# A message-passing layer on one core: the third chunk's lists merged at once, the last roots of the tail together, nine tiles fetched by rows, stores and list loads moved later on SyncE

## The chip, the cores and the metric

The kernel runs on one core of one Trainium2 chip. The metric is the device time of one execution in microseconds; the median over three executions is given, and one further execution was profiled. The engines are called PE (TensorE), DVE (VectorE), ACT (ScalarE), POOL (GpSimd) and SP (SyncE, which here only starts DMAs).

## The reference

A graph layer with a residual and a layer norm: 12,500 nodes, 400,000 edges sorted by target `dst`, 128 features, float32.

```python
# cut to what matters
rbf  = exp(-(distances[:, None] - centers) ** 2 / (2 * width * width))        # 50 centres
cut  = 0.5 * (cos(pi * distances / 10) + 1) * (distances <= 10)
W    = (silu(rbf @ fw1 + fb1) @ fw2 + fb2) * cut[:, None]
messages = (h[src] @ pw + pb) * W
agg  = segment_sum(messages, dst, num_segments=12500)
layer = h + (silu(agg @ mw1 + mb1) @ mw2 + mb2)
out  = layernorm(x + layer)                                                    # h is x
```

The weights of the edges are spread wide, so most edges lie beyond the distance of 10, have `cut` 0 and add nothing.

## The kernel before

**Packing.** The edges come in 7 chunks. For each chunk DVE finds which edges count and moves them together within a row by shifts that are doubled (`shift`, `moving`, `resting`: L509 to L519), and GpSimd scatters the rows into a DRAM area `packed` with one indirect DMA per chunk (L494). SyncE loads them back as lists of pairs (L821), and `unpack` merges the two halves of each pair on DVE (`two`, L839/840; `part`, L858; `f_src`, L869), turns them on PE (L902) and casts them to `srci`, the numbers of the source nodes for the gathers (L907), and likewise to `dl` and `cut`. The lengths go to DRAM (`near_d`, L896) and come back as `d`, ready for the radial basis (L1067). The kept edges fill 139 tiles of 512 edges (`NL`); chunk c holds the tiles from QB[c], with QB = (0, 13, 24, 46, 69, 91, 114, 141).

**The loop over tiles** (`octs`, from L1489). For tile q:
- `fetch` (L1048): GpSimd gathers four quarters of 128 rows of `proj` (the projected nodes, `h @ pw + pb`, in DRAM) with one indirect DMA each, into one of 21 buffers of the `quad` kind. It runs many tiles ahead of the rest where it can.
- `first` and `silu` (L1103, L1109), on PE and ACT, for two tiles at once; `second` (L1117, L1120) on PE.
- `message` (L1131) on DVE multiplies the gathered rows and PE's result.
- `place` (`hot`, L1143) on DVE builds a 0/1 matrix times `cut`, and `sum_up` (L1163) on PE adds up the messages by target; `add` (L1196) on DVE puts the sums into `aggT`.

In the tiles of `SINGLY` the first quarter isn't gathered: `one_by_one` lets SyncE read 32 row numbers at a time into registers (L1034) and copy each of the 128 rows by a DMA of its own (L1038, 0.5 KB) into one of four slots of `dl_0`; the message then takes two steps (L1129 for that quarter, L1131 for the rest). A_ROW is the pace, in us per row, at which these copies are written into the order.

**Finished nodes.** Blocks of up to 512 nodes go through `node_first` (L1204, L1205, then the silu L1209), `node_second` (L331, L334), `node_stats` (L1225 adds x, L1230 takes mean and variance), `deviations` (L1237 to L1241, a square root on ACT), `scales` (L1248, L1249) and `normalize` (L1260 on DVE, L1263 on ACT, then the store L173). Square root and silu lie in different table sets of ACT, so each change loads a table. Sixteen columns of statistics (four blocks) share one root.

**Order.** All engines run in order, and their order is written by hand: the generator keeps a model clock, the packing of later chunks is a coroutine that is woken when `awake[c]` has passed on that clock, and `pack_until` mixes its pieces in among the tiles. The end has its own script: `READY` says behind which tile a last block starts (block 80 nine tiles before the end, 84 six, 88 five, 90 three, 93 two, 95 last), and `keep_busy(n)` issues n matmuls that nobody uses into the bank of `ph` (L1352).

```python
READY = {80: 9, 84: 6, 88: 5, 90: 3, 93: 2}
...
            if q == NL - k:
                if t0 == 84:
                    keep_busy(8)
                node_first(t0)
```

Of the kernel before, what the change touches and what calls it, by code (L numbers as in the profile page):

```python
# [43 lines left out]
NL = 139  # L44
# [23 lines left out]
CLEAR_C = 2  # L68
PACK_US = 1.5
EARLY_US = 7  # L70
SINGLY = (22, 45, 62, 67, 86, 102, 118, 133)
A_ROW = .58
AT_ONCE = 32
FROM_BANK = 3

# [8 lines left out]
def kernel(  # L84
# [37 lines left out]
    nc = tc.nc  # L122
# [18 lines left out]

    x_sb, loaded = {}, [0]

    def load_x(t0, n=None):
        t = x4_sb[loaded[0] % X_BUFS]
        loaded[0] += 1
        node_dma(t0, t, x, False, n)
        x_sb[t0] = t
# [19 lines left out]
    def node_dma(t0, sb, dr, store, n=None, eng=nc.sync):  # L168

        for a, m, k in alike(rows(t0, n)):  # L170
            d = dr[(t0 + a) * P:(t0 + a) * P + m * k].rearrange("(p t) f -> p t f", p=k)
            s = sb[:k, a:a + m]
            eng.dma_start(d, s) if store else eng.dma_start(s, d)  # L173
# [164 lines left out]
    srci = keep.tile([P, NP, 2], I32, name="srci")  # L338
# [61 lines left out]
    clock = [3.2]  # L400
    pool = [0.0]
    there_at = {}
    summed = {}
    awake = [0.0] * NC_
# [49 lines left out]
    def parts(n):  # L454

        return [(a, b) for a, b in ((0, n // 16 * 16), (n // 16 * 16, n)) if b > a]
# [236 lines left out]
    def pack(c):  # L693
# [73 lines left out]
        for b in range(bits):  # L767
# [11 lines left out]
            n, k = reach(c, b, bits), 1 << b  # L779
            early = "two" not in pa_of  # L780
# [22 lines left out]
            yield one(n)  # L803

        yield from columns(c, nodes, r_d, first, 0, CAP, at_i)
        awake[c] = pool[0] + (2.2 if c == 1 else 3.0)
        awake[0] = 0.0
        yield 0
        yield from unpack(c)
# [1 line left out]
    def unpack(c):  # L811
# [15 lines left out]
        if c < 2:  # L827
            more_ = np_ if c == 0 else SPILL
            also = work.tile([P, 2, QE], F32, name="s", bufs=3).bitcast(I32)
            listed(also, 0, more_, 3, LISTS)  # L830
        awake[c] = max(awake[c], clock[0]) + (6 if c < 1 else 3.5 if c < 2 else 4.0)
        yield 0
        def alike_in(k):
            nc.vector.tensor_tensor(pair[:more_, :LISTS - 3, k::2], pair[:more_, :LISTS - 3, k::2],
# [2 lines left out]
        def one_of(to, k):  # L837

            nc.vector.tensor_tensor(to, pair[:np_, 0, k::2], pair[:np_, 1, k::2], OP.bitwise_or)  # L839
            nc.vector.tensor_tensor(to, to, pair[:np_, 2, k::2], OP.bitwise_or)  # L840
# [40 lines left out]
        def later(more=0.0):  # L881

            if c or known[0] >= DIRECT // QT:
                awake[c] = clock[0] + (5.0 if known[0] >= QB[c + 1] else 1.0 if c == 0 else 2.5) + more
                return 0.0
            return 0.5
# [3 lines left out]
        def lengths():  # L890

            if c < 2:
                alike_in(1)
            one_of(length, 1)
            for a, b in parts(np_):
                nc.sync.dma_start(near_d[p0 + a:p0 + b], length[a:b].bitcast(F32))  # L896
            stored.add(c)

        def to_places(f, to):
            t, tp = turned()  # L900
            for j in range(2):
                nc.tensor.transpose(tp[:, j, :np_], f[:, j * P:(j + 1) * P], ident[:np_, :np_])  # L902
            if to is srci:
                lengths()
                yield 1.4 if c < 2 else 0.8
            yield later(-2.0 if c == 1 and to is srci else 0.0)
            nc.vector.tensor_copy(to[:, p0:p0 + np_, :].rearrange("p r j -> p j r"),  # L907
                                  tp[:, :, :np_])
            back(t)
# [334 lines left out]
    def scales(group, both, s):  # L1244

        n = s.shape[1]
        r, by = (work.tile([P, 16], F32, name=k, bufs=2)[:, :n] for k in ("rs", "by"))
        nc.vector.reciprocal(r, s)  # L1248
        nc.vector.scalar_tensor_tensor(by, both[:, :, 0], -0.5, r, op0=OP.mult, op1=OP.mult)  # L1249
        at = 0  # L1250
        for t in group:
            ready.append((t, r[:, at:], by[:, at:]))
            at += len(rows(t))

    def normalize(t0, rs, by, on=(), eng=nc.sync):

        y = x_sb.pop(t0)
        for k, m in enumerate(rows(t0)):
            if k in on:
                nc.vector.tensor_scalar(y[:m, k, :], y[:m, k, :], rs[:m, k:k + 1], by[:m, k:k + 1],  # L1260
                                        op0=OP.mult, op1=OP.add)
            else:
                nc.scalar.activation(y[:m, k, :], y[:m, k, :], AF.Identity, bias=by[:m, k:k + 1],  # L1263
                                     scale=rs[:m, k:k + 1])
        node_dma(t0, y, out, True, eng=eng)

    ready = []

# [22 lines left out]
        begin[t0] = [at_q, at_q + 1, at_q + (4 if NODES + 24 < at_q < NL - 20 else 3)]  # L1291
        at_q += 2 if at_q % 4 == 1 else 3
    early = list(begin)
    assert begin[early[-1]][2] <= NL - 3

    def nodes(q):

        if deep:
            scales(*deep.pop())
        for _ in ready[:1 if q < NL - 6 else 2]:  # L1300
            normalize(*ready.pop(0))
        for k, t0 in enumerate(early):
            if begin[t0][0] - 5 == q:
                load_x(t0)
            if begin[t0][2] == q:
                if k % 4 == 0:
                    st_of[0] = statistics()
                node_stats(t0, st_of[0][:, k % 4 * 4:])
                if k % 4 == 3:
                    deep.append(deviations(early[k // 4 * 4:k + 1], st_of[0]))  # L1310
            if begin[t0][1] == q:
                node_second(t0)
            if begin[t0][0] == q:
                node_first(t0)
        for k, t0 in enumerate(TAIL):
            if q == NL - 9 + k:
                load_x(t0)
        if q == NL - 7:
            st_of[3] = statistics()
            node_stats(80, st_of[3])  # L1320
        if q == NL - 4:
            node_stats(84, st_of[3][:, 4:])
        if q == NL - 3:
            node_stats(88, st_of[3][:, 8:])
            dev_of.append(deviations([84, 88], st_of[3][:, 4:]))
            nc.scalar.activation(warm, half_pi, AF.Silu)
        if q == NL - 2:
            node_second(90)
            for k in (1, 2):
                st_of[k] = statistics()  # L1330
            scales(*dev_of.pop(0))
            for _ in (84, 88):
                normalize(*ready.pop(0))
# [3 lines left out]
    def tail(q):  # L1337

        for t0, k in READY.items():
            if q == NL - k:  # L1340
                if t0 == 84:
                    keep_busy(8)
                assert done_to(2 * added(q + 1)) >= (t0 + TAIL[t0]) * P
                node_first(t0)
            if q == NL - k + 1 and t0 in (80, 84, 88):
                node_second(t0)
# [142 lines left out]
    for q in range(NL - 1):  # L1489
# [39 lines left out]
        for k in now:  # L1529
            if q < NL - 2:  # L1530
                base_of(k, (1,))
            if q == NL - 7 and k == now[0]:
                deep.append(deviations([80], st_of[3]))
                nc.scalar.activation(warm, half_pi, AF.Silu)
            add(k)
# [24 lines left out]
    node_second(95)  # L1560
    early_dev = deviations([90, 93], st_of[1])
    node_stats(95, st_of[2], lambda: scales(*early_dev))
    last_dev = deviations([95], st_of[2])
    for _ in (90, 93):
        normalize(*ready.pop(0))
    scales(*last_dev)
    normalize(*ready.pop(0), on=(0, 1), eng=nc.scalar)

# [110 lines left out]
```

## Time and profile before

| | |
|---|---|
| median of 3 executions | 734.89 us (734.77 to 734.94) |
| profiled execution, its own time | 736.03 us |
| its span | 734.3 us |
| mean granted TensorE clock | 0.920 |
| DMA bytes moved, mean rate | 91.37 MB, 124 GB/s |

The span is the stretch that the profile covers, from the first to the last recorded instruction; 1.7 us of the profiled execution's time lie outside it. Its page gives for each engine the busy time, then slices of the span, the DMA queues, the chain of work that ended last, and the costliest groups of instructions. In a group's row the first number behind the bar is the busy time in us and the second the mean in ns of one; the number behind the second bar is the time in us that the engine stood idle just before these instructions, with what ended it (`issue`: nothing that the profile shows). A row of single instructions has the start, the duration, the engine, the line, what is written and read, how many follow each other, and in brackets the idle time before.

### The profile page before, as it was taken

The page shows a single profiled execution, that of the slowest core. Times are in us where ns is not written, and L with a number is a line of the kernel's source. Part 1 is how long each engine was busy: PE and PEld are TensorE (multiplying, and loading weights), DVE is VectorE, ACT ScalarE, POOL GpSimd, SP SyncE. Part 2 cuts the span into 40 slices and gives each one's busy share as a digit, 9 for nine tenths or more (in the row PEclk, how much of TensorE's full clock was granted, in tenths as well). Part 3 has the DMA queues.
Part 4 walks back from the last instruction along what each step waited for, and adds up shares of the span by engine and source line. Part 5 has one row for each costly group of instructions (what it writes and reads, how often), then busy time and mean ns, then how long its engine had stood idle before and what let it go on. Part 6 is the DMA issues. An engine that isn't in the chain of part 4 may idle for free.

```text
span 734.3 us, 13663 instructions
## 1 busy us (share of the span) xinstructions
PE 590.7 (80%) x3527; PEld 461.9 (63%) x3527; DVE 560.2 (76%) x1737; ACT 403.0 (55%) x574; POOL 533.5 (73%) x569
## 2 busy tenths in 40 slices
PE   6877876797888787878698969999978787778684
PEld 5766565676666665667476758777656565565463
DVE  8899798878878997989889957877455555556663
ACT  6557634274444864536457256859456644653763
POOL 7777777577777777777777777777777777777750
PEclk9999687999999998989989989999998999999886
DMA  8995442233234323343233343535333433343231
GB/s 267 313 318 189 143 128 73 89 120 99 76 110 128 95 85 101 99 127 88 83 111 113 96 134 97 155 120 151 110 113 94 127 124 98 98 142 116 79 114 53
DMA packets 53103, 91.37 MB, mean 124 GB/s; under 512 B 13824, under 2 KB 20576, under 8 KB 53018
## 3 DMA queue, kind: packets, MB, share of 16 engines
q1 hardware_dynamic: 34466, 53.20, 21.8%
q0 software_dynamic: 17840, 36.77, 18.1%
q8 instruction: 29, 0.48, 0.3%
q10 hardware_dynamic: 712, 0.46, 0.2%
q14 instruction: 56, 0.46, 0.2%
HBM read 74.59 MB, written 15.79 MB: 123 GB/s over the span
## 4 chain that ended last, share of the span: by engine, by line
DMA 13%; PE 13%; DVE 11%; POOL 9%; issue 6%; ACT 3%; DVEq 1%; POOLq 0%; SPq 0%; ACTq 0%
DMA quad<-proj,srci 11%; POOL quad L1048 9%; PE ph L1103 3%; PE bank L1120 3%; PE sums L1163 3%; DVE hot L1143 2%; DVE quad L1143 2%; PE bank L1205 1%; DVE msg L1131 1%; DMA pair<-packed 1%; DVE aggT L1196 1%; DVE st L1230 1%; DVEq L1173 1%; ACT x L1263 1%; DMA packed<-line,at_i 1%
## 5 line engine op out<-in xcount | busy, mean ns | idle before, releaser
L1048 POOL DMA_INDIRECT quad<-proj,srci x421 | 400.9, 952 | 132.5 <-issue 94.9
L1120 PEld LDWEIGHTS bank<-fw_sb,s 128*128 128x128 f32 x1112 | 159.7, 207 | 72.9 <-issue 65.8
L1109 ACT ACTIVATE s<-ph 128x1024 f32<-128x1024 f32 x70 | 71.2, 1017 | 179.7 <-PE ph L1103 179.5
L1120 PE MATMUL bank<-fw_sb,s 128*128 128x128 f32 x1112 | 159.7, 291 | 0.0
L1103 PE MATMUL ph<-rbf,w_sb 102*128 102x512 f32 x278 | 145.9, 651 | 6.7 <-ACT s L1109 3.5
L1163 PEld LDWEIGHTS sums<-hot,msg 128*128 128x128 f32 x816 | 107.6, 198 | 55.9 <-issue 27.5
L1143 DVE TENSOR_SCALAR hot<-iota_n,dl,cut 128x80 f32<-128x80 f32 (+4 forms) x408 | 109.1, 341 | 27.5 <-PE sums L1163 25.3
L1163 PE MATMUL sums<-hot,msg 128*128 128x80 f32 (+4 forms) x816 | 110.4, 280 | 14.2 <-DVE msg L1131 13.9
L1117 PE MATMUL bank<-fb_b,ones_b 96*128 96x512 bf16 x139 | 56.5, 406 | 54.8 <-DVE msg L1131 34.1
L1048 POOL DMA_INDIRECT x<-proj,srci x79 | 75.5, 955 | 24.2 <-issue 19.8
L1131 DVE TENSOR_TENSOR msg<-bank,quad 128x512 f32<-128x512 f32 (+1 forms) x82 | 55.5, 677 | 45.9 <-DMA quad<-proj,srci 41.6
L1103 PEld LDWEIGHTS ph<-rbf,w_sb 102*128 102x128 f32 x278 | 52.6, 211 | 46.1 <-issue 38.3
L1196 DVE TENSOR_TENSOR aggT<-aggT,sums 128x80 f32 (+4 forms) x209 | 53.9, 258 | 32.4 <-PE sums L1163 11.1
L1094 ACT ACTIVATE rbf<-d,rbf_bias,rbf_scale 102x512 f32<-102x512 f32 x70 | 56.3, 804 | 19.6 <-DMA d<-near_d 19.6
L1048 POOL DMA_INDIRECT quad<-in_x_dram,srci x48 | 46.7, 974 | 15.7 <-issue 11.9
L334 PEld LDWEIGHTS bank<-pw_sb,xT 128*128 128x128 f32 (+1 forms) x292 | 43.0, 212 | 9.4 <-issue 6.0
L1109 ACT ACT_TABLE_LOAD x36 | 46.2, 1283 | 0.6
L1095 ACT ACT_TABLE_LOAD x35 | 44.9, 1283 | 0.6
L1095 ACT ACTIVATE rbf<-rbf 102x512 f32<-102x512 f32 x70 | 44.1, 630 | 1.5
L334 PE MATMUL bank<-pw_sb,xT 128*128 128x128 f32 (+1 forms) x292 | 43.3, 296 | 0.7 <-ACT xT L984 0.6
L1163 PE MATMUL sums<-quad,quad 128*128 128x128 f32 (+3 forms) x296 | 40.8, 284 | 2.9 <-DVE quad L1131 2.8
L1143 DVE TENSOR_SCALAR quad<-iota_n,dl,cut 128x128 f32<-128x128 f32 (+3 forms) x148 | 40.6, 353 | 3.3 <-issue 2.1
(272 smaller groups left out, 791.4 us busy)
## 6 DMA issues: line engine op xcount, KB each, us to landing
d<-near_d SPq DMA_DIRECT2D x70, 256.0 KB
dl<-proj SPq DMA_DIRECT2D x1024, 0.5 KB
x<-in_x_dram SPq DMA_DIRECT2D x46, 256.0 KB
quad<-proj,srci POOLq DMA_INDIRECT x421
proj<-hp SPq DMA_DIRECT2D x24, 256.0 KB
out_dram<-x SPq DMA_DIRECT2D x22, 256.0 KB
r_d<-in_edge_weight_dram SPq DMA_DIRECT2D x5, 256.0 KB
r_dst<-in_dst_dram SPq DMA_DIRECT2D x5, 256.0 KB
```

Of the source, the lines that this page charges most:

```text
L334: nc.tensor.matmul(to[:m, k, :], lT[:, k * P:k * P + m], w, start=False, stop=(k == a + c - 1))
L1048: ins = nc.gpsimd.indirect_dma_start(out=got[:, j, :], out_offset=None, in_=proj if table is None else table, in_offset=bass.IndirectOffse ...
L1094: nc.scalar.activation(rbf[:u], d[:u], AF.Square, bias=rbf_bias[:u], scale=rbf_scale[:u])
L1095: nc.scalar.activation(rbf[:u], rbf[:u], AF.Exp, scale=-1.0 / (2.0 * width * width))
L1103: nc.tensor.matmul(ph[:, h, :], w1_sb[:2 * KR, h, :], rbf[:2 * KR], start=True, stop=True)
L1109: nc.scalar.activation(s[:, :n], ph[:, :n], AF.Silu)
L1117: nc.tensor.matmul(pu, ones_b[:, :P], bias_b["fb2"].rearrange("k j f -> k (j f)"), start=True, stop=False)
L1120: nc.tensor.matmul(pu[:, j * H:(j + 1) * H], s[:, j * P:(j + 1) * P], fw2_sb, start=False, stop=(j == QT - 1))
L1131: nc.vector.tensor_mul(msg[:, a:b, :], pu_of[q].rearrange("p (j f) -> p j f", j=QT)[:, a:b, :], got_of[q][:, a:b, :])
L1143: nc.vector.tensor_scalar(hot[:, j, :wide(q)], iota_n[:, :wide(q)], dl[:, at[0], at[1]], cut[:, at[0], at[1]], op0=OP.is_equal, op1=OP.mult)
L1163: ins = nc.tensor.matmul(pa[:, k * W:k * W + wide(q)], msg[:, j, :], hot[:, j, :wide(q)], start=(j % n == 0), stop=(j % n == n - 1))
L1196: nc.vector.tensor_add(to, to, pa[:, k * W:k * W + wide(q)])
```

## The change

1. `SINGLY` has nine tiles in place of eight, at other places: 22, 43, 58, 68, 83, 96, 109, 122, 136 for 22, 45, 62, 67, 86, 102, 118, 133. `A_ROW` goes from 0.58 to 0.515.
2. Chunk 2 is the third chunk. Its merge is woken as soon as its lists have been asked for (`awake` plus 0 in place of plus 4), and its `srci` is written 2.5 earlier on the model clock. In the order of DVE its `two`, `f_src`, `length` and `srci` now stand behind the first shift (L515) of chunk 3 and ahead of the message of tile 5, where they stood behind that tile's sums.
3. For chunks 3 to 6 the lists are loaded 8 later than the scatter on the model clock, not 3, and the lengths are stored behind the pause `later()`, not ahead of it. The scatters of chunks 3 to 6 move in POOL's order from ahead of the gathers (36,0), (52,0), (68,0), (82,0) (tile, quarter) to ahead of (38,0), (53,0), (68,1), (85,0). The merge of chunk 6 moves on DVE from behind the adds of tile 77's step to behind the message of tile 82.
4. The stores of normalised blocks, other than those of the last tiles, are kept in a list `to_store` and issued at the next step; `load_x` issues them first if it needs their buffer.
5. The statistics of the last four early blocks and those of block 80 get their roots behind each other, at tile 133, with one load of the root's table and one of silu's; block 80 is normalised later. The eight matmuls of `keep_busy` ahead of block 84 are gone.
6. At the very end block 90 is normalised on GpSimd (three instructions of 128x128) and block 93 on ACT ahead of block 95's root, not behind it.

```diff
@@ -68,8 +68,8 @@
 CLEAR_C = 2
 PACK_US = 1.5
 EARLY_US = 7
-SINGLY = (22, 45, 62, 67, 86, 102, 118, 133)
-A_ROW = .58
+SINGLY = (22, 43, 58, 68, 83, 96, 109, 122, 136)
+A_ROW = .515
 AT_ONCE = 32
 FROM_BANK = 3
 
@@ -141,8 +141,17 @@
 
     x_sb, loaded = {}, [0]
 
+    to_store = []
+
+    def store_all():
+
+        while to_store:
+            node_dma(*to_store.pop(0), out, True)
+
     def load_x(t0, n=None):
         t = x4_sb[loaded[0] % X_BUFS]
+        if any(v is t for _, v in to_store):
+            store_all()
         loaded[0] += 1
         node_dma(t0, t, x, False, n)
         x_sb[t0] = t
@@ -803,7 +812,7 @@
             yield one(n)
 
         yield from columns(c, nodes, r_d, first, 0, CAP, at_i)
-        awake[c] = pool[0] + (2.2 if c == 1 else 3.0)
+        awake[c] = pool[0] + (2.2 if c == 1 else 3.0 if c < 3 else 8.0)
         awake[0] = 0.0
         yield 0
         yield from unpack(c)
@@ -828,7 +837,7 @@
             more_ = np_ if c == 0 else SPILL
             also = work.tile([P, 2, QE], F32, name="s", bufs=3).bitcast(I32)
             listed(also, 0, more_, 3, LISTS)
-        awake[c] = max(awake[c], clock[0]) + (6 if c < 1 else 3.5 if c < 2 else 4.0)
+        awake[c] = max(awake[c], clock[0]) + (6 if c < 1 else 3.5 if c < 2 else 0.0 if c < 3 else 4.0)
         yield 0
         def alike_in(k):
             nc.vector.tensor_tensor(pair[:more_, :LISTS - 3, k::2], pair[:more_, :LISTS - 3, k::2],
@@ -892,6 +901,11 @@
             if c < 2:
                 alike_in(1)
             one_of(length, 1)
+            if c < 3:
+                store_lengths()
+
+        def store_lengths():
+
             for a, b in parts(np_):
                 nc.sync.dma_start(near_d[p0 + a:p0 + b], length[a:b].bitcast(F32))
             stored.add(c)
@@ -903,7 +917,9 @@
             if to is srci:
                 lengths()
                 yield 1.4 if c < 2 else 0.8
-            yield later(-2.0 if c == 1 and to is srci else 0.0)
+            yield later((0.0, -2.0, -2.5, *4 * (0.0,))[c] if to is srci else 0.0)
+            if to is srci and c >= 3:
+                store_lengths()
             nc.vector.tensor_copy(to[:, p0:p0 + np_, :].rearrange("p r j -> p j r"),
                                   tp[:, :, :np_])
             back(t)
@@ -1252,17 +1268,20 @@
             ready.append((t, r[:, at:], by[:, at:]))
             at += len(rows(t))
 
-    def normalize(t0, rs, by, on=(), eng=nc.sync):
+    def normalize(t0, rs, by, on=(), eng=nc.sync, v=nc.vector, soon=True):
 
         y = x_sb.pop(t0)
         for k, m in enumerate(rows(t0)):
             if k in on:
-                nc.vector.tensor_scalar(y[:m, k, :], y[:m, k, :], rs[:m, k:k + 1], by[:m, k:k + 1],
+                v.tensor_scalar(y[:m, k, :], y[:m, k, :], rs[:m, k:k + 1], by[:m, k:k + 1],
                                         op0=OP.mult, op1=OP.add)
             else:
                 nc.scalar.activation(y[:m, k, :], y[:m, k, :], AF.Identity, bias=by[:m, k:k + 1],
                                      scale=rs[:m, k:k + 1])
-        node_dma(t0, y, out, True, eng=eng)
+        if soon:
+            node_dma(t0, y, out, True, eng=eng)
+        else:
+            to_store.append((t0, y))
 
     ready = []
 
@@ -1291,14 +1310,15 @@
         begin[t0] = [at_q, at_q + 1, at_q + (4 if NODES + 24 < at_q < NL - 20 else 3)]
         at_q += 2 if at_q % 4 == 1 else 3
     early = list(begin)
-    assert begin[early[-1]][2] <= NL - 3
+    assert begin[early[-1]][2] == NL - 6
 
     def nodes(q):
 
-        if deep:
-            scales(*deep.pop())
+        while deep:
+            scales(*deep.pop(0))
+        store_all()
         for _ in ready[:1 if q < NL - 6 else 2]:
-            normalize(*ready.pop(0))
+            normalize(*ready.pop(0), soon=q >= NL - 6)
         for k, t0 in enumerate(early):
             if begin[t0][0] - 5 == q:
                 load_x(t0)
@@ -1306,7 +1326,7 @@
                 if k % 4 == 0:
                     st_of[0] = statistics()
                 node_stats(t0, st_of[0][:, k % 4 * 4:])
-                if k % 4 == 3:
+                if k % 4 == 3 and q != NL - 6:
                     deep.append(deviations(early[k // 4 * 4:k + 1], st_of[0]))
             if begin[t0][1] == q:
                 node_second(t0)
@@ -1338,8 +1358,6 @@
 
         for t0, k in READY.items():
             if q == NL - k:
-                if t0 == 84:
-                    keep_busy(8)
                 assert done_to(2 * added(q + 1)) >= (t0 + TAIL[t0]) * P
                 node_first(t0)
             if q == NL - k + 1 and t0 in (80, 84, 88):
@@ -1529,7 +1547,8 @@
         for k in now:
             if q < NL - 2:
                 base_of(k, (1,))
-            if q == NL - 7 and k == now[0]:
+            if q == NL - 6 and k == now[0]:
+                deep.append(deviations(early[-4:], st_of[0]))
                 deep.append(deviations([80], st_of[3]))
                 nc.scalar.activation(warm, half_pi, AF.Silu)
             add(k)
@@ -1560,9 +1579,9 @@
     node_second(95)
     early_dev = deviations([90, 93], st_of[1])
     node_stats(95, st_of[2], lambda: scales(*early_dev))
+    normalize(*ready.pop(0), on=(0, 1, 2), v=nc.gpsimd)
+    normalize(*ready.pop(0))
     last_dev = deviations([95], st_of[2])
-    for _ in (90, 93):
-        normalize(*ready.pop(0))
     scales(*last_dev)
     normalize(*ready.pop(0), on=(0, 1), eng=nc.scalar)
```

## The prediction, made before the changed kernel was run

> **What bounds the kernel now.** I read the page first, then the windows, then who waits for what inside each stretch, then single instructions around the places that the change touches. The page's head, its shares of engines and its groups for the gathers:
>
> ```profile
> span 734.3 us, 13663 instructions
> PE 590.7 (80%) x3527; PEld 461.9 (63%) x3527; DVE 560.2 (76%) x1737; ACT 403.0 (55%) x574; POOL 533.5 (73%) x569
> ...
> L1048 POOL DMA_INDIRECT quad<-proj,srci x421 | 400.9, 952 | 132.5 <-issue 94.9
> ...
> L1048 POOL DMA_INDIRECT x<-proj,srci x79 | 75.5, 955 | 24.2 <-issue 19.8
> ...
> L1048 POOL DMA_INDIRECT quad<-in_x_dram,srci x48 | 46.7, 974 | 15.7 <-issue 11.9
> ```
>
> PE shows the largest share and still isn't the bound. GpSimd issues 421 + 79 + 48 = 548 gathers of 128 rows, 0.95 us each; the 0.30 us between two of them is put down to "issue", so nothing holds it. In single instructions, and with the only long hole of the whole run:
>
> ```profile
> 130.54 1.00 POOL L1048 DMA_INDIRECT quad<-proj,srci  x1 [0.30 <-issue]
> 135.96 0.94 POOL L1048 DMA_INDIRECT quad<-proj,srci  x1 [4.42 <-DVE at_row L921]
> ...
> 488.38 0.95 POOL L1048 DMA_INDIRECT quad<-proj,srci  x1 [0.32 <-issue]
> 489.63 0.94 POOL L1048 DMA_INDIRECT quad<-proj,srci  x1 [0.30 <-issue]
> ```
>
> 489.63 − 488.38 = 1.25 us is the price of one gather, 5.0 us that of a tile of four. 548 x 1.25 = 685 us of the 734. Whether GpSimd sets the end too is read from the late tiles, by who makes DVE wait between 503 and 683 us (answer for the message line L1131):
>
> ```profile
>   DMA quad<-proj,srci: 63.1, 31
> ```
>
> 31 of the 38 messages there wait for their gathers, 63 us in all. So from tile 97 to tile 132 a microsecond that GpSimd gains or loses is one of the run. Ahead of that, tiles are limited by other engines and the gathers run ahead of their use; there a gain counts only if it lasts until tile 97. After tile 133 the tail has its own chain.
>
> **Third chunk at once (awake of chunk 2 at 0).** The hole costs 135.96 − 130.54 − 1.25 = 4.2 us. Its cause, on DVE and SyncE:
>
> ```profile
> 116.57 0.77 SPq L821 DMA_DIRECT2D pair<-packed  x2
> ```
>
> ```profile
> 120.20 0.68 DVE L515 TENSOR_SCALAR bank<-nodes 128x512 int32<-128x512 int32 x1
> ...
> 125.27 0.22 DVE L503 TENSOR_SCALAR at_f<-bank,end 128x1 f32<-128x1 f32 x1 [2.28 <-PE bank L729]
> ...
> 129.87 0.41 DVE L839 TENSOR_TENSOR two<-pair 44x256 int32<-44x256 int32 x1
> ...
> 135.44 0.25 DVE L907 CAST srci<-bank 128x88 int32<-128x88 f32 x1 [0.43 <-PE bank L902]
> ```
>
> The lists were asked for at 116.57 and are merged (`two`) only from 129.87, behind chunk 3's packing. With the change the merge stands directly behind the L515 that ended at 120.88, and the cast to `srci` ahead of the message of tile 5. Counting the same rows: the two merges, part and f_src take 1.6 us, then 2.1 us of packing and 0.9 us of lengths, and the cast, behind a transpose on PE that comes after the one that DVE waits 2.28 us for. So `srci` is written at about 126, where the gather needs it by 131.5. It is hidden with 5 us to spare; what is pushed back on DVE fills the 2.28 us it idles anyway. If the lists landed late, DVE would wait for them at 120.9 with the message of tile 5 behind it. A merge elsewhere (the 436.07 row below, whose lists were issued at 432.00) started 4 us after its issue, which would be 120.6 here. **Gain 4.2** (bounds 1.5 to 4.2: less, if the paces below catch).
>
> Does it last until tile 97? Two things could eat it: gathers waiting for a buffer whose message isn't done, and the consumer's stalls. The tightest buffer is that of the gather at 488.38 above, behind this message:
>
> ```profile
> 362.29 0.42 DVE L839 TENSOR_TENSOR two<-pair 46x256 int32<-46x256 int32 x1 [3.39 <-DMA pair<-packed]
> ...
> 436.07 0.42 DVE L839 TENSOR_TENSOR two<-pair 54x256 int32<-54x256 int32 x1 [7.17 <-DMA dl<-proj]
> ...
> 486.93 0.69 DVE L1131 TENSOR_TENSOR quad<-bank,quad 128x512 f32<-128x512 f32 x1
> ```
>
> The message ends at 487.62, 0.76 us before the gather. Gathers 4.2 us earlier need it at least 3.4 us earlier. The change provides that: lists of chunks 5 and 6 are loaded and merged later (+5 us in the written clock, `two` of chunk 6 five tiles on), so DVE no longer stands 3.39 and 7.17 us for them ahead of messages that could run. If only 7.17 goes, that is enough. The scatters move by one to three tiles among the gathers and stay as many. The stores of lengths behind `later()` and the blocks' stores a step on are queued on SyncE behind fewer unfinished waits; who needs them (the distances of tiles many steps on, a buffer of x that `load_x` flushes first) comes later, so they cost nothing.
>
> **One more tile by rows.** Nine first quarters instead of eight: 547 gathers, **−1.25**, at full worth since eight rather than seven lie ahead of tile 132. It is paid on SyncE:
>
> ```profile
> L1038 SPq DMA_DIRECT2D dl<-proj x1024: 227/228/400, 80.3 to 663.6; - x171
> ```
>
> ```profile
> 516.51 2.87 SPq L1038 DMA_DIRECT2D dl<-proj  x9
> ```
>
> ```profile
> SPq L173 <- ACT x L1263: 58.5, 17, 10.5
> ```
>
> 1024 rows in 583 us are 0.57 us each, the pace of the written order (A_ROW 0.58); unhindered, nine take 2.87 us, 0.32 each. At 0.515 instead of 0.58, 1152 rows end at 80 + 1152 x 0.57 x 0.515/0.58 = about 663. Message 135 comes at 693.9 by the sum below, that of tile 136, the last by rows, a tile later: about 698. The queue has room, and 58.5 us that it stood at stores are eased by the later store. Cost 0.
>
> **Last roots together, no keep_busy, block 80 later.** The tail's rows, from the message of tile 132:
>
> ```profile
> 682.63 0.69 DVE L1131 TENSOR_TENSOR msg<-bank,quad 128x512 f32<-128x512 f32 x1 [1.31 <-DMA quad<-proj,srci]
> ...
> 693.38 0.69 DVE L1131 TENSOR_TENSOR quad<-bank,quad 128x512 f32<-128x512 f32 x1
> ...
> 701.41 0.61 DVE L1196 TENSOR_TENSOR aggT<-aggT,sums 128x128 f32 x2 [5.24 <-PE bank L1205]
> ...
> 704.48 0.68 DVE L1131 TENSOR_TENSOR quad<-bank,quad 128x512 f32<-128x512 f32 x1
> ```
>
> ```profile
> 687.44 1.28 ACT L1241 ACT_TABLE_LOAD   x1
> 688.74 0.30 ACT L1241 ACTIVATE dev<-v,eps 128x4 f32<-128x4 f32 x1
> ...
> 692.10 1.28 ACT L1241 ACT_TABLE_LOAD   x1
> ...
> 695.02 0.60 ACT L1109 ACTIVATE s<-ph 128x512 f32<-128x512 f32 x1
> ```
>
> ```profile
> 695.66 3.57 PE L1352 MATMUL ph<-mb_b,ones_b 96*128 96x512 bf16 x8 [5.54 <-ACT s L1109]
> 699.03 0.63 PE L1204 MATMUL bank<-ones_b,mb_b 96*128 96x512 bf16 x1
> 699.46 1.91 PE L1205 MATMUL bank<-aggT,mw_sb 128*128 128x512 f32 x2
> 701.16 0.63 PE L1117 MATMUL bank<-fb_b,ones_b 96*128 96x512 bf16 x1
> 701.59 1.43 PE L1120 MATMUL bank<-fw_sb,s 128*128 128x128 f32 x8
> ```
>
> From message 132 to message 135 pass 21.85 us: two root loads, two Silu loads and four normalisations delay the silu at 695.02; keep_busy's eight matmuls write the bank that this silu reads, so PE stands 5.54, runs 3.57 of filler, and only then does block 84's first layer (699.03) and tile 135's second. With one root, PE no longer stands behind that silu: tile 133 has four gathers, so its message is at +5.0; tile 134's at about +10.4 (two tiles of gathers and DVE's small root operations; +10.75 before). Block 84's first layer follows at once; from its first row above to the start of tile 135's second pass 701.16 − 699.03 = 2.13 us, from there to message 135 another 704.48 − 701.16 = 3.32, and I add 0.85 because without the filler the slow rate will last longer (eight such matmuls took 1.43 above, 1.92 in the row of rival (b)): 10.4 + 2.13 + 3.32 + 0.85 = 16.7 instead of 21.85. **−5.1.** Three tiles of four gathers let message 135 come at +15.0 at the earliest, which bounds the gain at 6.85; what lies behind message 135 I take as unchanged, with the same matmuls and messages. The two table loads saved, 2.6 us, are inside this, not on top. The Trainium skill, ScalarE: Activation LUTs, "What ACT_TABLE_LOAD costs", adds a drain of about 1380 ns to the load's 1283. The trace agrees on the load, but the root starts 0.02 us after it (687.44 + 1.28, then 688.74), and Silu likewise; by the page the saving on ACT would be 5.3 us and, were all of it on the path, the sum 2.8 lower.
>
> **The end.**
>
> ```profile
> 726.57 0.30 ACT L1241 ACTIVATE dev<-v,eps 128x3 f32<-128x3 f32 x1 [1.79 <-DVE v L1240]
> ```
>
> ```profile
> 727.31 0.60 DVE L1260 TENSOR_SCALAR x<-x,rs,by 128x128 f32<-128x128 f32 x2
> ```
>
> ```profile
> 729.20 0.58 ACTq L173 DMA_DIRECT2D out_dram<-x  x1
> ```
>
> ```profile
> masks.py:199 POOL TENSOR_SCALAR_AFFINE_SELECT ident<-ident 128x128 f32<-128x128 f32 x1 | 0.3, 291 | 0.1
> ```
>
> Blocks 90 and 93 leave ACT's path behind the last root, so the last store is issued after DVE's two pieces, about 728.0 instead of 729.20: **−1.2**. GpSimd's three pieces for block 90 are not in the trace; the nearest row is 0.29 us for 128x128 on POOL, so I take 1 to 1.5 us for the three, inside the 1.79 that ACT waits for the last root and the time behind it; block 93's two on ACT fit into the same wait. At 2 us each on GpSimd they would end it about 2.5 us later. Bounds: −1.4 to +1.
>
> **Sum:** −4.2 − 1.25 − 5.1 − 1.2 = −11.75. The profiled execution took 736.03 (span 734.3 plus 1.7 outside): 724.3 there. The median of 734.89 is 1.1 below it: **723.1**.
>
> **Rivals.**
> (a) *The gathers' gain is eaten by buffers or by the consumer's pace.* For: 0.76 us at 488.38; the stall of 7.17 may come back in part, as the later lists are also loaded later. Against: both stalls are upstream of it. If half of 5.45 goes: 725.8; if all: 728.6.
> (b) *PE cold in the tail.* Without the filler PE idles up to message 134. The rows above show slow PE even behind the filler (0.85 us per pass of L1205). If three more tiles run their 8 second-layer and 8 sum matmuls at half speed:
>
> ```profile
> 717.20 1.92 PE L1163 MATMUL sums<-hot,msg 128*128 128x128 f32 x8
> ```
>
> that is about 2 us a tile, 6 us back: **729.1**. The Trainium skill, TensorE: Matmul & The Clock Gate, Part 1, says idling for about 3.4 us halves the clock and about 3.4 us of work restores it; the trace partly speaks against it, since 3.57 us of filler behind 5.54 idle didn't make 699.46 fast.
> (c) *Slower: SyncE doesn't keep the new pace.* The rows must average (698 − 80)/1152 = 0.536 us. If they stay at the 0.57 shown, because SyncE is held by loads and stores rather than by the order, tile 136's last row lands at 80 + 1152 x 0.57 = 737, 39 us late, and with everything behind it the end: **762**; at 0.55 it is 16 us late and ends at 739. It turns slower than before from 0.547. Against: 0.32 unhindered, waits of SyncE eased.
> (d) *The merge comes no earlier in effect*, because PE's transposes or the lists' landing hold `srci` to 135: the hole stays, **727.3**.
>
> **Numbers.** Forecast 0.54, (a) 0.15, (b) 0.13, (c) 0.10, (d) 0.08. Forecast's own range: 721.1 with the tail at −6.85 and the end at −1.4, to 725.9 with the tail at −3.5 and the end at 0. The range reaches up past (a), (b) and (d), with one of them joined by a late end, to 730.3, and down to 720.0; it leaves out (c) and two of them at once. 0.2% is 1.5 us, about what a measurement can tell from none. Faster: all but (c) and sliver mixes, 0.89; same 0.02; slower 0.09.
>
> **What would show it.** No interval above 2 us between gathers at 130 to 136; 547 gathers; waits of DVE at `two` of chunks 5 and 6 below 2 us; messages 97 to 132 still waiting for gathers; message 132 at 677.2; message 135 less than 18 us behind it; one root load between 680 and 700; last store about 0.7 us behind the last by. Wrong if DVE waits at L1129 for rows, GpSimd for buffers near tile 90, or PE passes take 0.85 us past message 135.

## The result: 725.94 us after 734.91, inside the range, with less gain than forecast

The changed kernel took 725.94 us (median of 4 runs, 721.87 to 726.96), the kernel before 734.91 (4 runs): a ratio of 0.9866 with an interval of 0.9828 to 0.9905. That is −9.0 us where −11.8 was forecast. The profiled execution is the slowest of the four, 726.96.

The page after, its head, its gathers and the group of the message:

```profile
span 725.2 us, 13905 instructions
PE 593.1 (82%) x3519; PEld 467.5 (64%) x3519; DVE 561.6 (77%) x1738; ACT 402.0 (55%) x570; POOL 532.8 (73%) x571
...
L1064 POOL DMA_INDIRECT quad<-proj,srci x419 | 398.3, 951 | 129.2 <-issue 101.6
...
L1064 POOL DMA_INDIRECT x<-proj,srci x80 | 76.1, 951 | 24.4 <-issue 19.5
...
L1147 DVE TENSOR_TENSOR msg<-bank,quad 128x512 f32<-128x512 f32 (+1 forms) x82 | 55.0, 671 | 37.5 <-DMA quad<-proj,srci 33.5
```

(Lines have moved: the gather is L1064, the message L1147, `two` L848, `srci` L923, the basis on ACT L1110, the sums L1179, the row copies L1054.) The bound is the same, GpSimd's gathers and messages that wait for them.

The span is best cut at the start of GpSimd's last gather: between 503 and 683 us 31 of 38 messages waited for gathers before and 29 of 38 after, so what GpSimd gains there shows at its last gather. The start of that gather, and behind it the last pass of the sums of tile 138, in the kernel before:

```profile
708.85 0.95 POOL L1048 DMA_INDIRECT quad<-proj,srci  x1 [0.30 <-issue]
```

```profile
718.91 1.31 PE L1163 MATMUL sums<-quad,quad 128*128 128x128 f32 x8
```

and after the change, with the three new GpSimd instructions:

```profile
705.16 0.94 POOL L1064 DMA_INDIRECT quad<-proj,srci  x1 [0.30 <-issue]
716.88 1.31 POOL L1276 TENSOR_SCALAR x<-x,rs,by 128x128 f32<-128x128 f32 x3 [10.78 <-issue]
```

```profile
703.62 0.91 PE L1221 MATMUL bank<-aggT,mw_sb 128*128 128x384 f32 x2 [2.50 <-DVE aggT L1212]
...
709.11 1.91 PE L1179 MATMUL sums<-quad,quad 128*128 128x128 f32 x8
```

The last gather starts 3.7 us sooner (708.85 to 705.16); the sums of 138 end 5.9 behind it in place of 11.4, another 5.5; from there to the end of the span it is 14.1 and 14.2. So 3.7 + 5.5 − 0.1 = 9.1 = 734.3 − 725.2.

**The hole is gone.** Gathers and DVE around 130 us, after:

```profile
130.14 0.94 POOL L1064 DMA_INDIRECT quad<-proj,srci  x1 [0.30 <-issue]
131.39 0.94 POOL L1064 DMA_INDIRECT quad<-proj,srci  x1 [0.30 <-DVE bank L524]
132.64 0.94 POOL L1064 DMA_INDIRECT quad<-proj,srci  x1 [0.30 <-issue]
```

```profile
122.60 0.44 DVE L848 TENSOR_TENSOR two<-pair 44x256 int32<-44x256 int32 x1 [0.40 <-DMA pair<-packed]
...
127.18 0.25 DVE L923 CAST srci<-bank 128x88 int32<-128x88 f32 x1 [0.29 <-PE bank L916]
127.35 0.69 DVE L1147 TENSOR_TENSOR msg<-bank,quad 128x512 f32<-128x512 f32 x1
```

Gathers follow at 1.25 us throughout; `srci` is written 4 us ahead of its need, and DVE waits 0.40 us for the lists.

**What took its place.** GpSimd has new, short waits, one early and others at the gathers of tiles 82, 84 and 86:

```profile
69.42 0.94 POOL L1064 DMA_INDIRECT quad<-in_x_dram,srci  x1 [2.20 <-PE bank L343]
...
424.89 0.94 POOL L1064 DMA_INDIRECT quad<-proj,srci  x1 [0.86 <-PE sums L1179]
...
434.23 0.94 POOL L1064 DMA_INDIRECT quad<-proj,srci  x1 [0.82 <-DVE msg L1147]
...
445.89 0.94 POOL L1064 DMA_INDIRECT quad<-proj,srci  x1 [0.66 <-issue]
```

Beyond the usual 0.30 these are 1.9 and 0.56 + 0.52 + 0.36 = 1.4 us. Two of the second group wait for work of DVE and PE on earlier tiles, which is the wait for buffers of rival (a); the third is put to `issue`. Messages were late: that of tile 77 came at 433.28, where it came at 426.06 before. What held them up, the waits view suggests, after:

```profile
ACT rbf L1110 <- DMA d<-near_d: 33.6, 15, 5.6
DVE two L848 <- DMA pair<-packed: 7.5, 3, 5.2
```

and before:

```profile
ACT rbf L1094 <- DMA d<-near_d: 19.6, 9, 4.3
```

ACT waits 14 us more for the distances `d`, which SyncE loads between the row copies. DVE still stands 5.2 us for the lists of chunk 5, and 1.9 for those of chunk 4; chunk 6's stall of 7.2 went.

**The tail.** Messages 132 and 135, and block 84's first layer:

```profile
679.25 0.69 DVE L1147 TENSOR_TENSOR msg<-bank,quad 128x512 f32<-128x512 f32 x1 [1.57 <-DMA quad<-proj,srci]
...
693.95 0.69 DVE L1147 TENSOR_TENSOR quad<-bank,quad 128x512 f32<-128x512 f32 x1 [0.40 <-DMA quad<-proj,srci]
```

```profile
688.91 1.13 PE L1221 MATMUL bank<-aggT,mw_sb 128*128 128x512 f32 x2 [1.95 <-DVE aggT L1212]
```

14.7 us lie between the messages where 21.85 did, and message 135 now waits 0.40 us for its gather: up to here the tail has gone over from ACT's table loads and the filler to GpSimd. From message 135 to the end of the sums it is 17.1 us, where it was 15.7.

### The profile page after: what moved, and what is told of

Read it like the earlier page. It is cut to its first block, busy times and chain, and to the rows that moved or that the text cites. A ratio compares the mean times of both kernels' runs of the same rounds, so it can differ in the third digit from the quotient of the medians.

```text
span 725.2 us, 13905 instructions
## 1 busy us (share of the span) xinstructions
PE 593.1 (82%) x3519; PEld 467.5 (64%) x3519; DVE 561.6 (77%) x1738; ACT 402.0 (55%) x570; POOL 532.8 (73%) x571
## 5 line engine op out<-in xcount | busy, mean ns | idle before, releaser
L1064 POOL DMA_INDIRECT quad<-proj,srci x419 | 398.3, 951 | 129.2 <-issue 101.6
L1136 PEld LDWEIGHTS bank<-fw_sb,s 128*128 128x128 f32 x1112 | 161.4, 209 | 62.2 <-issue 54.0
L1136 PE MATMUL bank<-fw_sb,s 128*128 128x128 f32 x1112 | 161.6, 293 | 0.0
L1119 PE MATMUL ph<-rbf,w_sb 102*128 102x512 f32 x278 | 148.2, 660 | 10.9 <-ACT s L1125 7.5
L1179 PEld LDWEIGHTS sums<-hot,msg 128*128 128x128 f32 x816 | 110.6, 201 | 42.8 <-issue 27.5
L1179 PE MATMUL sums<-hot,msg 128*128 128x80 f32 (+4 forms) x816 | 111.4, 281 | 3.5 <-DVE msg L1147 3.4
L1064 POOL DMA_INDIRECT x<-proj,srci x80 | 76.1, 951 | 24.4 <-issue 19.5
L1147 DVE TENSOR_TENSOR msg<-bank,quad 128x512 f32<-128x512 f32 (+1 forms) x82 | 55.0, 671 | 37.5 <-DMA quad<-proj,srci 33.5
L1110 ACT ACTIVATE rbf<-d,rbf_bias,rbf_scale 102x512 f32<-102x512 f32 x70 | 56.3, 804 | 33.7 <-DMA d<-near_d 33.6
L1064 POOL DMA_INDIRECT quad<-in_x_dram,srci x48 | 47.2, 984 | 17.1 <-issue 11.6
L1179 PE MATMUL sums<-quad,quad 128*128 128x128 f32 (+3 forms) x296 | 42.1, 289 | 3.7 <-DVE quad L1147 3.7
L1147 DVE TENSOR_TENSOR quad<-bank,quad 128x512 f32<-128x512 f32 (+2 forms) x40 | 25.5, 639 | 23.5 <-DMA quad<-proj,srci 23.5
```

The costliest lines, as they stand in the source:

```text
L1064: ins = nc.gpsimd.indirect_dma_start(out=got[:, j, :], out_offset=None, in_=proj if table is None else table, in_offset=bass.IndirectOffse ...
L1110: nc.scalar.activation(rbf[:u], d[:u], AF.Square, bias=rbf_bias[:u], scale=rbf_scale[:u])
L1119: nc.tensor.matmul(ph[:, h, :], w1_sb[:2 * KR, h, :], rbf[:2 * KR], start=True, stop=True)
L1136: nc.tensor.matmul(pu[:, j * H:(j + 1) * H], s[:, j * P:(j + 1) * P], fw2_sb, start=False, stop=(j == QT - 1))
L1147: nc.vector.tensor_mul(msg[:, a:b, :], pu_of[q].rearrange("p (j f) -> p j f", j=QT)[:, a:b, :], got_of[q][:, a:b, :])
L1179: ins = nc.tensor.matmul(pa[:, k * W:k * W + wide(q)], msg[:, j, :], hot[:, j, :wide(q)], start=(j % n == 0), stop=(j % n == n - 1))
```

## The experiments

Chips differ, so each kernel is compared with the kernel before on its own chip. On three chips every kernel, the one before too, has medians of 1.02 to 1.04 ms; those runs stand at the end of this section, apart.

| kernel | median, us | kernel before there | ratio | interval |
|---|---|---|---|---|
| the change | 725.94 | 734.91 | 0.9866 | 0.9828 to 0.9905 |
| only the roots | 730.50 | 736.68 | 0.9923 | 0.9885 to 0.9961 |
| the change with eight tiles by rows | 725.14 | 737.48 | 0.9836 | 0.9810 to 0.9862 |
| the same and filler ahead of block 90 | 723.41 | 737.67 | 0.9814 | 0.9788 to 0.9840 |

**Only the roots, on the kernel before.**

```diff
-        if deep:
-            scales(*deep.pop())
+        while deep:
+            scales(*deep.pop(0))
-                if k % 4 == 3:
+                if k % 4 == 3 and q != NL - 6:
-                if t0 == 84:
-                    keep_busy(8)
-            if q == NL - 7 and k == now[0]:
+            if q == NL - 6 and k == now[0]:
+                deep.append(deviations(early[-4:], st_of[0]))
```

> The kernel before with only the tail's part, where the kernel before takes 735 us: the roots of the last four early blocks and of block 80 behind each other at tile 133, and no eight filler matmuls ahead of block 84. Theory: message 135 comes 15 to 17 us behind message 132 instead of 21.85, so 728.0 to 729.8. Rival (matmuls stay slow without the filler): 733 to 736. Rival (the whole gain is here): 726.

−6.2 us in the medians. That is the size expected against a kernel before of 735 us, though 730.50 itself lies above the 728.0 to 729.8 named, since the kernel before took 736.68 on this chip; both rivals are out. Its profile: messages 132 and 135; the two long waits of GpSimd and the last gather; the last sums.

```profile
684.81 0.69 DVE L1131 TENSOR_TENSOR msg<-bank,quad 128x512 f32<-128x512 f32 x1 [1.37 <-DMA quad<-proj,srci]
...
698.46 0.69 DVE L1131 TENSOR_TENSOR quad<-bank,quad 128x512 f32<-128x512 f32 x1
```

```profile
68.92 0.94 POOL L1048 DMA_INDIRECT quad<-in_x_dram,srci  x1 [2.19 <-PE bank L982]
...
137.08 0.94 POOL L1048 DMA_INDIRECT quad<-proj,srci  x1 [4.88 <-DVE at_row L921]
...
710.94 0.94 POOL L1048 DMA_INDIRECT quad<-proj,srci  x1 [0.30 <-issue]
```

```profile
713.35 1.35 PE L1163 MATMUL sums<-quad,quad 128*128 128x128 f32 x8
```

Message 135 is 13.65 us behind 132, sooner than the 15 to 17 expected (tile 133 is fetched by rows in this kernel and has three gathers), and the sums end 3.8 behind the last gather, not 11.4: the tail alone is worth 7.6 here. How that divides between the roots and the filler, which were taken out together, no run tells apart. The run as a whole shows less, because its last gather starts 2.1 later than in the first profile of the kernel before (the hole is 0.5 longer, and GpSimd has an early wait like the one at 69 us above). That early wait is thus no work of the change: this kernel has the early code of before.

**Eight tiles by rows.** `SINGLY` and `A_ROW` of the kernel before, the rest as changed. So the number of tiles, their places and the pace of the copies go back together.

> The changed kernel with the eight tiles by rows and the pace of before (0.58). Where the kernel before takes 735 us, theory: one gather more is +1.25, less SyncE work ahead of the loads of d gives back up to 1.4 of waits for buffers, so the whole lies 0 to 1.5 above the changed kernel and the last gather at 705 to 707. Where SyncE's stream is slow and every kernel takes about 1020 us, theory: the copies hold up the loads of d, ACT waits less for them than with nine tiles, and the ratio to the kernel before falls from 1.005 to 0.98 to 0.995. Rival (SyncE's load has no part in it): the ratio there stays at 1.00 to 1.01.

The ratio is 0.9836 against 0.9866, and the intervals overlap: the ninth tile, with its places and pace, brings nothing that shows. The expectation was 0 to 1.5 us above the change; by the ratios it is 2.2 below. Its part on the chips of 1.02 ms stays untested. The last gather; the first layer of block 90 and the last sums; ACT's wait for `d`; the message of tile 84:

```profile
706.98 0.94 POOL L1064 DMA_INDIRECT quad<-proj,srci  x1 [0.30 <-issue]
```

```profile
704.39 1.65 PE L1221 MATMUL bank<-aggT,mw_sb 128*128 128x384 f32 x2 [2.19 <-DVE aggT L1212]
...
708.91 1.79 PE L1179 MATMUL sums<-hot,msg 128*128 128x128 f32 x8
710.53 1.06 PE L1179 MATMUL sums<-quad,quad 128*128 128x128 f32 x8
```

```profile
ACT rbf L1110 <- DMA d<-near_d: 4.1, 3, 2.2
```

```profile
450.74 0.68 DVE L1147 TENSOR_TENSOR msg<-bank,quad 128x512 f32<-128x512 f32 x1
```

The same message in the changed kernel:

```profile
460.14 0.68 DVE L1147 TENSOR_TENSOR msg<-bank,quad 128x512 f32<-128x512 f32 x1
```

ACT's wait for `d` falls from 33.6 to 4.1 us, DVE's longest wait for lists at `two` from 5.2 to 1.5, the message of tile 84 comes 9.4 us sooner, and GpSimd's waits at the gathers of tiles 82, 84 and 86 are gone. The last gather starts 1.8 us later. Of that, 1.25 is the price of the extra gather; GpSimd's waits come out nearly even, with 3.5 us in two early ones here (2.44 and 1.66 us, each with the usual 0.30) and 1.9 early and 1.4 later in the change. Behind the last gather the sums end in 4.6 us against 5.9: slow matmuls reach the last pass of the sums in the change (1.91), and only the pass ahead of it here (1.79, then 1.06). One tile more by rows takes 1.25 from GpSimd and, by these traces, gives about as much back.

**Filler where it helps.** To the last kernel, six filler matmuls ahead of block 90's first layer:

```diff
             if q == NL - k:
+                if t0 == 90:
+                    keep_busy(6)
                 assert done_to(2 * added(q + 1)) >= (t0 + TAIL[t0]) * P
```

> The version that the runs point to: eight tiles by rows at the pace of before, the rest of the change, and six filler matmuls ahead of block 90's first layer, where PE stood 2.2 to 2.5 us in the tail and the matmuls behind ran at the slow rate (1.79 to 1.92 for eight sums). Theory: that stretch runs fast (eight sums in 1.05 to 1.2), sums of tile 138 end about 1.3 sooner behind the last gather, and the whole is 0.7 to 2 below the run with eight tiles alone (725.1; ratio to the kernel before 0.981 to 0.983). Rival (the stretch stays slow, or the last gather's landing sets the end): 725 to 726.5, ratio 0.983 to 0.985.

```profile
698.17 1.46 PE L1372 MATMUL ph<-mb_b,ones_b 96*128 96x512 bf16 x6
...
700.63 0.91 PE L1221 MATMUL bank<-aggT,mw_sb 128*128 128x384 f32 x2 [0.83 <-DVE aggT L1212]
...
703.43 1.05 PE L1179 MATMUL sums<-hot,msg 128*128 128x128 f32 x8
...
706.08 0.49 PE L1179 MATMUL sums<-quad,quad 128*128 128x128 f32 x2 [0.76 <-DVE quad L1147]
```

```profile
703.20 0.94 POOL L1064 DMA_INDIRECT quad<-proj,srci  x1 [0.30 <-issue]
```

PE stands 0.83 us instead of 2.19, the eight sums behind take 1.05 instead of 1.79, and the last sums now wait for their message, 3.4 us behind the last gather. That is the expected stretch at the fast rate: the granted clock from 700 to 706 us is 1.00, where it is 0.51 from 704.4 to 711.0 in the change. It is one profile with the filler, against four without it (the kernel before, the change, only the roots, eight tiles) that all have a slow stretch here. 723.41, ratio 0.9814: below both kernels by its median. Its interval lies wholly below 1, and overlaps those of the change and of eight tiles alone, so that it beats them is likely, and not settled across chips. GpSimd had no long early wait in this profile, and its last gather is the earliest of all with 548 of them.

**How much of the hole reaches the last gather.** These two kernels and only the roots make the same 548 gathers as the kernel before. From the last gather ahead of the hole (at 130.54 in the kernel before) to the last of all it is 578.31 us there and 579.80 with only the roots; in the two kernels with the merge at once and eight tiles it is 574.74 and 573.71, and behind 136 us no gather of theirs waits longer than 0.32. So in these two the hole's 4.1 us, 4.42 less the usual 0.30, are not taken up again. In the change it is 573.77 with one gather fewer.

**The chips where everything takes 1.02 to 1.04 ms.** Four kernels ran there: the change again, the change with the third chunk's merge at its old place, the change with the lists of chunks 3 to 6 at their old place, and only the roots. The edits:

```diff
# merge late
-(6 if c < 1 else 3.5 if c < 2 else 0.0 if c < 3 else 4.0)
+(6 if c < 1 else 3.5 if c < 2 else 4.0)
-(0.0, -2.0, -2.5, *4 * (0.0,))[c]
+(0.0, -2.0, 0.0, *4 * (0.0,))[c]
# lists early
-        awake[c] = pool[0] + (2.2 if c == 1 else 3.0 if c < 3 else 8.0)
+        awake[c] = pool[0] + (2.2 if c == 1 else 3.0)
# ... and store_lengths() at the end of lengths() for every chunk
```

> The changed kernel once more, to see why its four runs lie between 721.9 and 727.0. Theory (GpSimd's chain sets the end): median 725 to 726, again spread over 4 to 5 us, and a profile whose time differs from the first by x us shows last gathers that start earlier by about x, because single waits of GpSimd ahead of tile 90 (2.2 us at 69 us and some 0.4 to 0.6 us each at tiles 81 to 85 in the first profile) come and go. Rival (the tail's matmul clock): the last gather stays at 705.2 within 0.5 us and the difference lies behind it.

> The changed kernel with the third chunk's merge where it was before (awake plus 4.0, no earlier srci). Theory: a hole of 3 to 5.5 us between gathers near 130 us returns; GpSimd sets the end, and fewer waits for buffers near tile 82 give back at most 2 of it: 728.0 to 730.0. Rival (the hole would have been taken up by waits later on, and the gain is the tail's alone): at most 726.5.

> The changed kernel with the lists of chunks 3 to 6 loaded as before (3 behind the scatter, lengths stored ahead of the pause). The prediction's step: DVE stands 3.4 and 7.2 us for lists again, messages before tile 90 come late, gathers wait for buffers: 727 to 730. Rival (the late lengths made the messages of tiles 66 to 77 3 to 7 us late, through ACT waiting for d, and that caused the waits for buffers): 722.5 to 724.5, and ACT's wait for d falls from 33.6 to about 20 us.

The later ones expected the same against the changed kernel:

> The changed kernel with the third chunk's merge where it was before, where the kernel before takes 735 us. Theory: a hole of 3 to 5.5 us between gathers near 130 us returns; the last gather starts 2.5 to 4.5 us later than the changed kernel's 705.2, what lies behind it stays near 20 us, and the whole is 727.5 to 730.0. Rival (the hole would have been taken up by waits later on, and the gain is the tail's alone): the last gather within 1 us of 705.2 and the whole at most 726.5.

> The changed kernel with the lists of chunks 3 to 6 loaded as before (3 behind the scatter, lengths stored ahead of the pause). The prediction's step: DVE stands 3.4 and 7.2 us for lists again, messages before tile 90 come late, gathers wait for buffers: 1.5 to 4 us above the changed kernel. Rival (the late lengths made the messages of tiles 66 to 77 3 to 7 us late, through ACT waiting for d, and that caused the waits for buffers): 1.5 to 3.5 us below the changed kernel, and ACT's wait for d falls from 33.6 to about 20 us.

| ratio to the kernel before | first chip | second chip | third chip |
|---|---|---|---|
| the change | 1.0059 (1.0021 to 1.0096) | 1.0048 (1.0011 to 1.0085) | |
| merge late | 1.0112 and 1.0136 | 1.0160 (1.0104 to 1.0216) | 1.0102 (1.0056 to 1.0147) |
| lists early | 0.9884 (0.9815 to 0.9952) | 1.0031 (0.9995 to 1.0067) | |
| only the roots | 0.9917 (0.9865 to 0.9969) | | |

The change is no gain there. Its profile on the first of them, the page's head, ACT's wait, and SyncE in one stretch:

```profile
span 1019.7 us, 13905 instructions
```

```profile
ACT rbf L1110 <- DMA d<-near_d: 91.7, 15, 16.3
```

```profile
824.22 10.18 SPq L1054 DMA_DIRECT2D dl<-proj  x10
834.52 0.38 SPq L182 DMA_DIRECT2D out_dram<-x  x1
834.95 0.53 SPq L1083 DMA_DIRECT2D d<-near_d  x1
```

Ten row copies take 10.2 us where nine took 2.9 in the kernel before, the load of `d` stands behind them, and ACT waits 91.7 us in all for such loads. These waits aren't what the change adds: with only the roots, 0.9917 on the same chip, they are 102.1. GpSimd stands for much more than the usual 0.30 there, up to 19.5 us at one gather, so its gathers don't follow each other as they do at 735. The late merge lies above the change by its ratio on both chips where both ran, clear of the change's interval on the second only. Its traces do show what the merge's place does. At the first gather of tile 24, where the hole stood, GpSimd waits 13.5 to 13.9 us behind DVE in all four profiles with the late merge and in that of only the roots; in the four with the merge at once, of the change and of the lists early, it waits 3.8 to 3.9, behind ACT. So the hole is the late merge's work, and not what it is worth at 735. The lists' place made no difference on the second chip; on the first the ratio rests on two runs and the median, 1030.9, lies above the kernel before's 1026.36, so it is unclear. What makes SyncE slow on these chips no run tells apart. The times at 735 of the late merge and of the early lists stay untested, and so does why the change's four runs lie 5 us apart.

## Why the prediction was right, and where it wasn't

- **Bound: right.** From tile 97 on most messages wait for gathers, 29 of 38 between 503 and 683 us, and now some do to tile 138.
- **Third chunk, −4.2: right in the trace.** The hole is gone and nothing stands in its place near 130 us; `srci` came at 127.2, not 126. The late merge alone brings the hole back, which its traces on the slow chips show; with eight tiles by rows all of it reaches the last gather. Its worth in the whole time was not measured at 735 us, since the kernel with the late merge ran only on the slow chips.
- **That the gain lasts to tile 97: partly.** Rival (a) came true for 1.4 us. The step that failed is "DVE no longer stands 3.39 and 7.17 us": chunk 5's stall grew to 5.2. With eight tiles by rows and the same late lists it is 1.5, so it failed through the row copies.
- **One more tile by rows, "Cost 0": wrong.** The rows were sized against their own due time, where they did have room (the last of the 1152 was issued at 675, its message came at 699). They were not weighed against what stands in the same queue behind them: the loads of `d` and of the lists. ACT's wait for `d` is 4.1 us with eight tiles and 33.6 with nine, with the message of tile 84 9.4 us later, and the whole is no better than with eight. Whether the ninth tile, the places or the faster pace does it wasn't separated.
- **Roots and filler, −5.1: right in kind, too small.** Message 135 came at +14.7 instead of +16.7. The 0.85 us added for a slow PE was not needed: the pass at 688.91 took 1.13 us where 1.91 stood before. "What lies behind message 135 I take as unchanged" failed: it grew from 15.7 to 17.1 us. At the sums of 138 the gain behind the last gather was 5.5 in the change and 7.6 alone; PE's slow stretch, granted clock 0.51 to 0.55, lasted 6.6 us in the change and 3.5 with only the roots.
- **Rival (b), PE cold: right one block later, at about 2 us, not 6.** After 2.50 us of idling ahead of block 90 the matmuls ran slow (eight sums in 1.91), and with six fillers they took 1.05. The Trainium skill, TensorE: Matmul & The Clock Gate, Part 1, puts the idle time that slows PE at about 3.4 us; here shorter gaps were enough: slow matmuls followed 2.19, 2.36 and 2.50 us, and in the kernel before 1.95, so the slow stretch is no work of the change:

```profile
713.75 0.91 PE L1205 MATMUL bank<-aggT,mw_sb 128*128 128x384 f32 x2 [1.95 <-DVE aggT L1196]
```

  The length of the gap alone doesn't decide, though: the other gap of 1.95 us, at 688.91 in the change, and one of 2.88 us at 586.14 there were followed by matmuls at the full clock.
- **The end, −1.2: mis-sized, about 0.** Two of DVE's four small steps ahead of the last root, then the root and the last stores, after:

```profile
717.31 0.20 DVE L1253 TENSOR_TENSOR dif<-st 128x3 f32<-128x3 f32 x1
...
717.54 0.24 DVE L1255 SCALAR_TENSOR_TENSOR dif<-dif 128x3 f32<-128x3 f32 x1
```

```profile
718.11 0.30 ACT L1257 ACTIVATE dev<-v,eps 128x3 f32<-128x3 f32 x1 [0.50 <-DVE v L1256]
...
719.48 1.06 ACTq L182 DMA_DIRECT2D out_dram<-x  x2
```

  GpSimd's three pieces took 1.31 us, inside the 1 to 1.5 taken. The last store, the second of these two, starts 1.8 us behind the last root, where 2.6 lay between (726.57 and 729.20 before). But the root itself comes 7.1 us behind the end of the sums, not 6.35, and the prediction had left that stretch as it was. Of the 0.74, 0.2 lie at the first layers behind the sums, where PE is still slow, 0.4 ahead of DVE's adding of x, most of it a wait of 0.31 that the profile puts to `issue`, and 0.1 at DVE's small steps beside GpSimd (0.16 each in the kernel before). Block 93 on ACT is not the cause, since the root waits 0.50 for DVE behind it. With eight tiles the root comes 6.50 behind. The Trainium skill, GPSIMD Engine Reference, section 1 (Specifications), says that GpSimd shares its SBUF interface with VectorE and contends with DVE instructions of two SBUF inputs; the two rows above agree in kind, one of the four steps doesn't show it (0.16 in both kernels), and it is a tenth of a microsecond.
- **The sum.** Forecast −5.45 at the last gathers and −6.3 behind: −3.7 and −5.4 came. Against the 1.75 missing in the first stand new waits of 1.9 and 1.4 us; a smaller early wait of the kernel before and GpSimd's somewhat shorter instructions make up the difference. The early wait comes and goes in kernels of both kinds (2.20 in the change, 2.19 with only the roots, none of that size with the last kernel), and is perhaps a part of why the four runs spread over 5 us; the fastest of them, 721.87, left no trace. That the total came near is in part luck: message 135 came 2.0 us sooner behind message 132 than forecast, which made up for the longer stretch behind it, and the time lies by the 725.8 of rival (a) although waits for buffers cost only 1.4.

## What to carry to other kernels

A copy that has room ahead of its own use can still be late for its neighbours: whoever gives a queue more work must look at what stands behind it and who waits for that, not at the queue's total. Cut a span at the last instruction of the engine that bounds it: what lies ahead and behind can then be compared between runs whose totals drift by more than the effect. And look where filler matmuls stand: eight of them ran for 3.57 us directly in front of a waiting layer, and the kernels without them, which also have one root load fewer there, were faster; six stood in a gap in which PE waited 0.83 us even behind them, so they held up nothing.

## What the runs showed of the hardware that was not expected

- The kernel before took 1.02 to 1.03 ms in the median on three chips and 0.73 to 0.74 on the others; SyncE's row copies (10 in 10.2 us, against 9 in 2.9) and a lower granted TensorE clock (0.79 against 0.91) are what the profiles show of it.
- PE can fall to about half its granted clock after only 1.95 to 2.5 us of idling, and stay there for 3.5 us (716.0 to 719.5 in the kernel before, 0.51) or 6.6 us (704.4 to 711.0 in the changed kernel, 0.51); a gap of 2.88 us at 586.14 in the changed kernel was followed by 1.00.
- A GpSimd `tensor_scalar` of 128x128 float32 took 0.44 us, DVE's 0.34 in the same kernel.
